# A transformer block in float32 on one core: the down projection as seven products of quarters, with its weights looked up one stage earlier

## The chip, the cores and the metric

The kernel runs on one core of a Trainium2 chip. The time is device microseconds of that core for one execution of the whole block. Before the change it was 3123.69 us (median of 3 runs, 3119.15 to 3126.1).

## What is computed

One block over 2048 tokens of width 1024: causal attention with 16 heads and rotary embedding, then a gated feed-forward part whose three weight matrices are stored as 4-bit codes with one scale for each 64 columns. The change touches the feed-forward part alone:

```python
NF4 = [-1.0, -0.6962, -0.5251, -0.3949, -0.2844, -0.1848, -0.0911, 0.0,
       0.0796, 0.1609, 0.2461, 0.3379, 0.4407, 0.5626, 0.7230, 1.0]
H, I = (1024, 2752)
W = (NF4[codes].reshape(out, in_ // 64, 64) * scales[:, :, None]).reshape(out, in_)
gate = einsum('bsh,ih->bsi', x, Wg)
up = einsum('bsh,ih->bsi', x, Wu)
inter = silu(gate) * up
return einsum('bsi,hi->bsh', inter, Wd)
...
x = x + layernorm(attention(layernorm(x)))
x = x + layernorm(ffn(layernorm(x)))
```

## The kernel before

All data are float32. A product of two float32 matrices is made of three matmuls on rounded parts (`mm3`, lines 114 to 116): each operand is split into a high and a low part (`split`: ACT copies the high part, DVE subtracts to get the low one, line 121), and high x high, high x low and low x high are added in one PSUM bank. Every such matmul is 128 x 128 by 512 columns.

The stages follow each other: queries, keys and values with attention; the output projection (`project_out`), whose rows go out to `yd` and come back to be transposed (`fill_x2`) into the four groups `x2[0..3]` of 512 tokens that stay in SBUF; gate and up; down. There are eight PSUM banks, taken in turn with `any_bank`. SBUF is cut into slots by tag (`SLOTS`): `hd` 7, `w` 3, `xc` 4, `pa` 6 of 8 KB for each partition, and `pb` 2, `f4` 4, `pw` 3, `t2` 3, `ol` 1 of 4 or 2 KB. All DMAs are issued by SP, in order. The order of the instructions on each engine is made by a scheduler when the program is built; a tile waits until a slot of its tag is free.

*Gate and up.* The 2752 inner columns are 22 tiles of 128 (`NIT`), the last of 64. One round handles one tile: `gate_up` runs over the four token groups, each with a gate product and an up product of 24 matmuls, then ACT makes Silu, DVE multiplies, the result is split, and high and low part together are stored in DRAM (`ind`). Beside that, `gate_up_weights` makes the weights of the next round in four calls of `looked_up`, into two tiles of `hd` or `pa`, so that two rounds' weights exist at a time. The last two rounds run together, group by group.

*The lookup.* `looked_up` turns 128 x 512 codes into values without a table: seven straight lines, each an ACT instruction (line 498) into a `t2` slot, an eighth line on DVE (line 493), and minima and maxima of them on DVE (lines 503 to 510), then the product with the scales (line 511). It takes 7 ACT and 10 DVE instructions, and loads of codes and scales into a `pw` slot.

*Down.* For each half of the output columns and each half of the tokens, eight banks gather eight token tiles over 22 steps (`kt`). A step loads one tile of `ind` (1 MB, `load_inter`) and multiplies it with one tile of looked-up down weights (`wd`), which are made beside these products (`down_weights`) and kept for the second token half. The last step leaves one matmul of each three out where its 64 rows hold both parts. Then `keep` copies a bank to SBUF on ACT. When both column halves of a token tile are there, `finish` loads the residual row `x1d`, makes the layer norm (bn_stats, bn_aggr and small operations on DVE, a power on GpSimd, ACT and DVE for the rows) and stores the result. In the last quarter the final four steps (`LAST`) are run bank by bank, so that `finish` of one bank lies beside the matmuls of the next.

Of the kernel before, what the change touches and what calls it, by code (L numbers as in the profile page):

```python
# [28 lines left out]
NIT = 22  # L29
EPS = 1e-5  # L30
# [12 lines left out]
L0 = (0.30380719900131226, -1.0)  # L43
L2 = (0.1301555633544922, 0.2558603286743164)
L4 = (0.09966795146465302, 0.11423042416572571)
L6 = (0.09105003625154495, 0.09105003625154495)
L8 = (0.08134990185499191, 0.07958029955625534)
L10 = (0.0918029397726059, 0.06250642240047455)
L12 = (0.12190717458724976, -0.046918854117393494)
L14 = (0.2770431637763977, -0.9393021464347839)  # L50
# [7 lines left out]
def block_kernel(ctx, tc, x, wq, wk, wv, wo, gu_codes, gu_scales, d_codes, d_scales, cos_sin, out):  # L58
# [41 lines left out]
    for ab in (L2, L4, L6, L8, L10, L12, L14):  # L100
        bias_of[ab] = const.tile([P, 1], F32, tag=f"b{len(bias_of)}", name="bias")
        G.memset(bias_of[ab], ab[1])
# [20 lines left out]
    def ln_stats(row):  # L123
        st = small.tile([P, 2, 6], F32, tag="st", name="st")
        for i in range(2):
            V.bn_stats(st[:, i, :], row[i])  # L126
        mv = small.tile([P, 2], F32, tag="mv", name="mv")
# [32 lines left out]
    ind = [[dram.tile([P, 2, 2, 512], F32, tag=f"ind{g}_{k}", name=f"ind{g}_{k}") for k in range(NIT)] for g in range(2)]  # L160
# [320 lines left out]
    def looked_up(codes, s0, s1, rows, tags=None):  # L481
# [10 lines left out]
        l0 = slot("ol" if not tags else "t2", [P, 512], F32, "l0")  # L492
        V.tensor_scalar(l0, c8.bitcast(I32), L0[0], L0[1], ALU.mult, ALU.add)
        V.tensor_scalar(c8, c8.bitcast(I32), 1.0, -8.0, ALU.mult, ALU.add)

        def line(ab):
            ln = slot("t2", [P, 512], F32, "ln")
            A.activation(ln, c8, AF.Identity, bias=bias_of[ab], scale=ab[0])  # L498
            return ln

        mp = slot("f4", [P, 2, 512], F32, "mp")
        m, p = mp[:, 0], mp[:, 1]
        V.tensor_tensor(m, l0, line(L2), ALU.min)
        V.tensor_tensor(m, m, line(L4), ALU.min)  # L504
        V.scalar_tensor_tensor(m, line(L6), 0.0, m, ALU.min, ALU.min)
        l8 = line(L8)
        V.tensor_tensor(p, l8, line(L10), ALU.max)
        V.tensor_tensor(p, p, line(L12), ALU.max)
        V.tensor_tensor(p, p, line(L14), ALU.max)
        V.scalar_tensor_tensor(m, p, 0.0, m, ALU.max, ALU.add)  # L510
# [3 lines left out]
    def gate_up_weights(it, tags=None):  # L514
        w = it_cols(it)
        wt = [slot(tag, [P, 2, 4, w], FR, "wt") for tag in ("hd", "pa" if it % 2 else "hd")]
# [30 lines left out]

    def gate_up(it, wt, w, c):
        g = any_bank()
        hl = slot("pb", [P, 2, 512], FR, "hl")  # L550

        def product(o, a):
            for k in range(KE):
                mm3(o, wt[k // 4][:, :, k % 4, a : a + P], x2[c][k], k == 0, k == KE - 1)

        product(g, 0)
        rows = P if w == 256 else D
        inter, hi = f32(hl[:rows, 1, :]), hl[:rows, 0, :]
        if w == 256:
            u = any_bank()  # L560
            product(u, P)
        else:
            u = f32(hi)
            A.copy(u, g[D:P, :])
        A.activation(inter, g[:rows], AF.Silu)
        V.tensor_tensor(inter, u, inter, ALU.mult)
        split(hi, hl[:rows, 1, :], inter)
        load(ind[c // 2][it][:rows, c % 2], f32(hl[:rows]))

    for it in range(NIT):  # L570
        if it < NIT - 2:
            for c in range(NC):
                gate_up(*todo[it], c)
        if it + 1 < NIT:
            now, steps = gate_up_weights(it + 1)
            todo.append(now)
            for step in steps:
                step()
    for c in (1, 0, 2, 3):
# [4 lines left out]
    WD_TAGS = (  # L584
        ["pa"] * 4 + ["w"] * 3 + ["pa"] + ["xc"] * 3,
        ["pa", "xc"] + ["pa"] * 4 + ["w"] * 3 + ["pa", "xc"],
    )
    LAST = 4
    SECOND = 16
    XT_TAGS = ["f4"] * 4 + ["pb"] * 2 + ["pw"] * 2  # L590
    wd = {}

    def down_weights(n, kt):

        ns = slice(n * 512, (n + 1) * 512)
        if kt % 2 == 0:
            t = slot(WD_TAGS[n][kt // 2], [P, 2, 2, 512], FR, "wd")
            wd[n, kt], wd[n, kt + 1] = t[:, :, 0], t[:, :, 1]
        t = wd[n, kt]
        rows = P if kt < NIT - 1 else D  # L600
        b1 = min(2 * kt + 1, 42)
        m = looked_up(
            d_codes[kt * P : kt * P + rows, ns], d_scales[2 * kt : 2 * kt + 1, ns], d_scales[b1 : b1 + 1, ns], rows
        )
        if rows == P:
            split(t[:, 0], t[:, 1], m)
        else:
            A.copy(t[:, 0], m)
            V.tensor_tensor(t[D:, 0], m[D:], f32(t[D:, 0]), ALU.subtract)

    def load_inter(g, kt):
        t = slot("hd", [P, 2, 2, 512], FR, "it")
        if kt < NIT - 1:
            load(f32(t), ind[g][kt])
        else:
            for a in range(2):
                load(f32(t[a * D : (a + 1) * D]), ind[g][kt][:D])
        return t

    def down(o, it_, w, tt, first, last):  # L620

        i = it_[:, tt // 4, :, tt % 4 * P : (tt % 4 + 1) * P]
        if not last:
            mm3(o, i, w, first, False)
        else:
            T.matmul(o, lhsT=i[:, 0], rhs=w[:, 0], start=False, stop=False)
            T.matmul(o, lhsT=i[:, 1], rhs=w[:, 0], start=False, stop=True)

    def keep(t, o, n):

        if t % 4 == 0:
            kept.setdefault(n, []).append(slot(("hd", "xc")[n], [P, 4, 512], F32, "kept"))
        return A.copy(kept[n][t // 4][:, t % 4], o)

    def finish(t, left, right):

        xt = slot(XT_TAGS[t % 8], [P, E], F32, "xt")
        load(xt, x1d[t * P : (t + 1) * P, :])
        _, rs, nb = ln_stats((left, right))
        for src, h in ((right, slice(512, E)), (left, slice(0, 512))):  # L640
            A.activation(xt[:, h], xt[:, h], AF.Identity, bias=nb)
            V.scalar_tensor_tensor(xt[:, h], src, rs, xt[:, h], ALU.mult, ALU.add)
            load(out[t * P : (t + 1) * P, h], xt[:, h])

    kept = {}
    last = None
    left = [(n, kt) for n in range(2) for kt in range(NIT)]

    def make(upto):
        while left and 2 * NIT - len(left) < upto:  # L650
            down_weights(*left.pop(0))

    for n in range(2):
        for g in range(2):
            os = [any_bank() for _ in range(8)]
            final = n == 1 and g == 1
            its = []
            for kt in range(NIT):
                if (n, g) == (0, 0):
                    make(kt + 1)  # L660
                elif (n, g) == (0, 1):

                    with tc.issue_after(last.ins):
                        make(NIT + min(4 + kt, SECOND))
                it_ = load_inter(g, kt)
                if final and kt >= NIT - LAST:
                    its.append(it_)
# [67 lines left out]
```

## Time and profile before

The profiled execution took 3127.5 us; its span from the first to the last instruction is 3125.7 us.

| what | value |
|---|---|
| busy: TensorE, weight loads, DVE, ACT, GpSimd | 3003.9, 2470.5, 2161.1, 1831.5, 702.8 us |
| mean granted TensorE clock | 0.982 |
| first and last matmul of gate and up (starts) | 1692.5, 2643.2 us |
| first and last matmul of down (starts) | 2643.4, 3116.4 us |
| end of the span | 3125.7 us |
| DMA traffic of the whole span | 552.31 MB, mean 177 GB/s |

How to read it: an engine's busy time is the time in which at least one of its instructions was running. Matmuls overlap each other, so their mean duration is longer than the distance from one to the next, and that distance is what a matmul costs. A row of the profile gives line, engine, operation, written and read tiles, shapes and count, then busy time and mean duration, then how long the engine had been idle before these instructions and what ended the idle time.

### The profile page before, as it was taken

Reading aid. Unit: us, or ns where it says so; the run is one execution under the profiler, and the core shown is the slowest. Engines: PE = TensorE matmul, PEld = TensorE weight load, DVE = VectorE, ACT = ScalarE, POOL = GpSimd, SP = SyncE. Lnnn points to the kernel's source line nnn. Section 1 sums busy time; section 2 is a strip of 40 time slices with the busy share of each in tenths; the row PEclk is TensorE's granted clock in tenths of the full one; section 3 lists DMA queues with packets and bytes.
Section 4 is the critical chain, followed back from the end, with each engine's and each line's share of the span. In section 5 each row is a group of like instructions: output and inputs, shape, how many; then the busy total and the mean of one; then the engine's idle time right before and its main releaser. Section 6 shows DMA issues by size and latency. Waiting matters only on the chain.

```text
span 3125.7 us, 43392 instructions
## 1 busy us (share of the span) xinstructions
PE 3003.9 (96%) x14656; PEld 2470.5 (79%) x14656; DVE 2161.1 (69%) x4428; ACT 1831.5 (59%) x3846; POOL 702.8 (22%) x888
## 2 busy tenths in 40 slices
PE   7979999999998999989988999999999999999998
PEld 6868888787877787778767888888888888888887
DVE  7457778687777777776574987666776669868322
ACT  3246667676766666676554876555665558657211
POOL 5344344343433443454222000000000000000000
PEclk9989999999999999999989999999999999999999
DMA  8777666557547656462355332222322226867785
GB/s 312 250 234 224 209 207 197 178 163 222 181 161 191 200 191 196 165 202 67 113 186 193 122 128 95 93 90 102 103 99 90 93 101 213 278 218 246 254 305 197
DMA packets 246495, 552.31 MB, mean 177 GB/s; under 512 B 20224, under 2 KB 110336, under 8 KB 219136
## 3 DMA queue, kind: packets, MB, share of 16 engines
q1 hardware_dynamic: 246272, 549.53, 53.8%
q8 instruction: 116, 1.90, 0.3%
q14 instruction: 107, 0.88, 0.1%
HBM read 403.70 MB, written 145.75 MB: 176 GB/s over the span
## 4 chain that ended last, share of the span: by engine, by line
PE 42%; DMA 3%; DVE 3%; ACT 1%; issue 1%; SPq 0%; DVEq 0%; POOLq 0%; POOL 0%; ACTq 0%
PE bk L114 13%; PE bk L116 13%; PE bk L115 13%; DMA cs<-in_d_codes 1%; DMA out<-xt 1%; PE pj L440 0%; PE pj L441 0%; PE pj L442 0%; DMA it<-ind 0%; DMA y<-yd 0%; DVE mp L511 0%; DMA cs<-in_d_scales 0%; PE pt L148 0%; DVE st L126 0%; DVE mp L504 0%
## 5 line engine op out<-in xcount | busy, mean ns | idle before, releaser
L498 ACT ACTIVATE ln<-cs,bias 128x512 f32<-128x512 f32 x910 | 611.8, 719 | 136.0 <-DVE mp L504 38.4
L114 PE MATMUL bk<-x,wt 128*128 128x512 f32 x1376 | 535.8, 390 | 0.0
L115 PE MATMUL bk<-x,wt 128*128 128x512 f32 x1376 | 535.4, 389 | 0.0
L116 PE MATMUL bk<-x,wt 128*128 128x512 f32 x1376 | 535.2, 389 | 0.0
L284 POOL TENSOR_SCALAR prob<-prob,rc 128x512 f32<-128x512 f32 (+3 forms) x640 | 408.1, 660 | 408.9 <-DVE rc L279 245.2
L262 ACT ACTIVATE prob<-s,mxs 128x512 f32<-128x512 f32 (+3 forms) x640 | 401.4, 630 | 161.2 <-DVE mxs L261 147.0
L121 DVE TENSOR_TENSOR pw<-pt,pw 128x512 fp32r<-128x512 f32 (+3 forms) x640 | 377.8, 602 | 135.1 <-ACT pw L120 133.4
L261 DVE TENSOR_REDUCE mxs<-s 128x1 f32<-128x512 f32 (+3 forms) x640 | 380.1, 602 | 96.3 <-PE s L257 57.7
L120 ACT CAST pw<-pt 128x512 fp32r<-128x512 f32 (+3 forms) x640 | 323.5, 526 | 165.4 <-PE pt L294 134.7
L132 POOL TENSOR_TENSOR rs<-ve,nhalf 128x1 f32<-128x1 f32 x64 | 40.0, 637 | 1552.2 <-DVE ve L130 1546.3
L294 PE MATMUL pt<-ident,prob 128*128 128x128 f32 x2176 | 347.1, 276 | 5.1 <-DVE pw L121 4.8
L294 PEld LDWEIGHTS pt<-ident,prob 128*128 128x128 f32 x2176 | 267.8, 142 | 59.3 <-issue 7.5
L255 PE MATMUL s<-k,q 128*128 128x512 f32 (+3 forms) x640 | 266.8, 417 | 36.9 <-ACT prob L262 35.4
L115 PEld LDWEIGHTS bk<-x,wt 128*128 128x128 f32 x1376 | 258.6, 188 | 53.9
L114 PEld LDWEIGHTS bk<-x,wt 128*128 128x128 f32 x1376 | 258.7, 188 | 53.5
L116 PEld LDWEIGHTS bk<-x,wt 128*128 128x128 f32 x1376 | 258.4, 188 | 53.7
L114 PE MATMUL bk<-wd,it 128*128 128x512 f32 x672 | 261.6, 389 | 1.2 <-DMA it<-ind 1.2
L115 PE MATMUL bk<-wd,it 128*128 128x512 f32 x672 | 261.4, 389 | 0.0
L116 PE MATMUL bk<-wd,it 128*128 128x512 f32 x672 | 261.3, 389 | 0.0
L299 PE MATMUL o<-pw,v 128*128 128x512 f32 (+3 forms) x640 | 250.6, 394 | 4.9 <-DVE pw L121 4.6
L298 PE MATMUL o<-pw,v 128*128 128x512 f32 (+3 forms) x640 | 247.1, 387 | 6.1 <-ACT pw L120 5.5
L114 PE MATMUL qkv<-xc,w 128*128 128x512 f32 x576 | 235.8, 409 | 13.0 <-ACT w L173 7.4
(124 smaller groups left out, 5514.2 us busy)
## 6 DMA issues: line engine op xcount, KB each, us to landing
xc<-xd SPq DMA_DIRECT2D x96, 1024.0 KB, 8.8
it<-ind SPq DMA_DIRECT2D x84, 1024.0 KB, 7.0
ind<-hl SPq DMA_DIRECT2D x84, 512.0 KB, 2.6
q<-qs SPq DMA_DIRECT2D x128, 256.0 KB, 7.1
cs<-in_gu_scales SPq DMA_DIRECT2D x172, 128.0 KB, 3.1
cs<-in_gu_codes SPq DMA_DIRECT2D x86, 256.0 KB, 2.9
tab<-in_cos_sin SPq DMA_DIRECT2D x32, 512.0 KB, 9.8
xd<-xr SPq DMA_DIRECT2D x16, 1024.0 KB, 6.8
```

Source lines behind the costliest of these rows:

```text
L114: r = T.matmul(o, lhsT=w[:, 0], rhs=xx[:, 0], start=first, stop=False)
L115: T.matmul(o, lhsT=w[:, 0], rhs=xx[:, 1], start=False, stop=False)
L116: T.matmul(o, lhsT=w[:, 1], rhs=xx[:, 0], start=False, stop=last)
L120: A.copy(hi, src)
L121: V.tensor_tensor(lo, src, f32(hi), ALU.subtract)
L255: mm = T.matmul(s, lhsT=q[:, 0, j * P : (j + 1) * P], rhs=k[:, b:e], start=True, stop=False)
L261: V.tensor_reduce(mx, s, AX.X, ALU.max, negate=True)
L262: A.activation(prob[i][:, j, : e - b], s, AF.Exp, bias=mx, accum_out=sums[:, j % BATCH, i : i + 1])
L284: G.tensor_scalar(p, p, rc[:, jj % BATCH, i : i + 1], 0.0, ALU.mult, ALU.add)
L294: T.transpose(pt[:, j * P : (j + 1) * P], prob[kb // 4][:, j, kb % 4 * P : (kb % 4 + 1) * P], ident)
L299: T.matmul(o[:, cs], lhsT=v[:, kb, :], rhs=pw[:, 1, cs], start=False, stop=kb == nk - 1)
L498: A.activation(ln, c8, AF.Identity, bias=bias_of[ab], scale=ab[0])
```

## The change

1. *Down as seven products of quarters (Strassen's scheme in Winograd's form).* The tokens are split by 512-token groups (even, odd), the inner tiles into tiles 0 to 10 and 11 to 21, the output columns into two halves of 512. Instead of eight products of quarters there are seven, of sums of quarters (`PRODUCTS`), each with 11 steps over eight banks. Results are gathered in SBUF quarters `u`, `c`, `v`, `d` (`evict`), partly on ACT, partly by DVE additions that read PSUM, partly by GpSimd additions.
2. *The operands are made in the gate-up stage.* Rounds alternate between tiles k and k + 11 (`PAIRS`), so that after each second round the four quarters of one k are there. GpSimd makes S1 to S4 from them, unsplit, and SP stores A11, A12, A22 and S1 to S4 in DRAM (`aq`). The quarters wait in `pb` and `f4` slots.
3. *All down weights are looked up beside gate and up*, two lookups in each round; GpSimd makes T1 to T4, and SP stores B11, B21, B22 and T1 to T4 in DRAM (`bq`). The room for them is in `f4`.
4. *In down*, `fetch` loads each step's A tile (512 KB, `f4`), and B tiles two steps at a time (512 KB, `pb`), and splits them (ACT and DVE) into `hd` and `w` slots.
5. *The lookup* has five ACT lines, three of them with two slopes (Prelu), and six DVE instructions.
6. *finish* takes bn_stats of the quarter that was complete early beforehand, and one of the two row additions goes to GpSimd. The upper rows (n = 5) use the three `pw` slots for the residual rows, the lower rows (n = 6) pairs in `xc`.

Three products have a last step of 64 rows; the matmuls are of the same length.

```diff
+PAIRS = [k // 2 + k % 2 * (NIT // 2) for k in range(NIT)]
...
+PRODUCTS = (("A11", "B11"), ("A12", "B21"), ("S2", "T2"), ("S3", "T3"), ("S1", "T1"), ("S4", "B22"), ("A22", "T4"))
...
-        l0 = slot("ol" if not tags else "t2", [P, 512], F32, "l0")
-        V.tensor_scalar(l0, c8.bitcast(I32), L0[0], L0[1], ALU.mult, ALU.add)
         V.tensor_scalar(c8, c8.bitcast(I32), 1.0, -8.0, ALU.mult, ALU.add)
         def line(ab):
             ln = slot("t2", [P, 512], F32, "ln")
-            A.activation(ln, c8, AF.Identity, bias=bias_of[ab], scale=ab[0])
+            if ab[2] == 1.0:
+                A.activation(ln, c8, AF.Identity, bias=bias_of[ab], scale=ab[0])
+            else:
+                A.activation(ln, c8, AF.Prelu, bias=bias_of[ab], scale=ab[0], alpha=ab[2])
             return ln
...
+        low = line(CODES_6_8)
+        V.scalar_tensor_tensor(m, line(CODES_9_12), CODES_9_12[3], low, ALU.add, ALU.max)
+        V.scalar_tensor_tensor(m, line(CODES_2_5), CODES_2_5[3], m, ALU.add, ALU.min)
+        V.tensor_tensor(m, m, line(CODES_0_1), ALU.min)
+        V.scalar_tensor_tensor(m, line(CODES_13_15), CODES_13_15[3], m, ALU.add, ALU.max)
         V.tensor_tensor(m, m, sc, ALU.mult)
...
 def gate_up(it, wt, w, c):
...
+        kt, later, grp, odd = it % half, it // half, c // 2, c % 2
+        if (kt, later, grp) not in rooms:
+            rooms[kt, later, grp] = slot("f4" if later else "pb", [P, 2, 512], F32, "in")
+        inter = rooms[kt, later, grp][:, odd]
...
-        split(hi, hl[:rows, 1, :], inter)
-        load(ind[c // 2][it][:rows, c % 2], f32(hl[:rows]))
+        if (later, odd) != (0, 1):
+            keep(("A11", "A12", "A22")[later + odd], inter)
+        first = rooms[kt, 0, grp]
+        if later == 0 and {(kt, grp, 0, 1 - odd)} <= have:
+            s3 = slot("ol", [P, 512], F32, "s3")
+            G.tensor_tensor(s3, first[:, 0], first[:, 1], ALU.subtract)
+            keep("S3", s3)
+        if {(kt, grp, a, b) for a in range(2) for b in range(2)} <= have:
+            second = rooms[kt, 1, grp]
+            G.tensor_tensor(first[:, 1], first[:, 1], second[:, 1], ALU.add)
+            keep("S1", first[:, 1])
+            G.tensor_tensor(first[:, 0], first[:, 1], first[:, 0], ALU.subtract)
+            keep("S2", first[:, 0])
+            G.tensor_tensor(second[:, 0], second[:, 0], first[:, 0], ALU.subtract)
+            keep("S4", second[:, 0])
...
+    for n in range(NIT):
+        if n < NIT - 2:
+            for c in range(NC):
+                gate_up(*todo[n], c)
+        if n + 1 < NIT:
+            now, steps = gate_up_weights(n + 1)
...
+        for j in range(2):
+            down_weights(n // 2, 2 * (n % 2) + j)
...
+    def fetch(a, b, kt):
+        st = slot("f4", [P, 2, 512], F32, "ast")
+        load(st, aq[a][kt])
+        ta = slot("hd", [P, 2, 2, 512], FR, "at")
+        split(ta[:, 0], ta[:, 1], st)
+        if kt % 2 == 0:
+            n = min(2, half - kt)
+            st = slot("pb", [P, 2, 512], F32, "bst")[:, :n]
+            load(st, bq[b][:, kt : kt + n])
+            b_tile[b] = slot("w", [P, 2, 2, 512], FR, "bt")
+            split(b_tile[b][:, 0, :n], b_tile[b][:, 1, :n], st)
+        return ta, b_tile[b][:, :, kt % 2]
...
+    def finish(r, lower, known, fresh, xt):
+        t = 8 * (r // 4) + 4 * lower + r % 4
+        load(xt, x1d[t * P : (t + 1) * P, :])
+        st = early_stats[known, r]
+        known, fresh = quarter[known][r], quarter[fresh][r]
+        V.bn_stats(st[:, 1, :], fresh)
+        _, rs, nb = ln_rest(st)
+        a, b = (slice(512, E), slice(0, 512)) if lower else (slice(0, 512), slice(512, E))
+        A.activation(xt[:, b], xt[:, b], AF.Identity, bias=nb)
+        A.activation(known, known, AF.Identity, bias=nb, scale=rs)
+        V.scalar_tensor_tensor(xt[:, b], fresh, rs, xt[:, b], ALU.mult, ALU.add)
+        (V if lower and r == 7 else G).tensor_tensor(xt[:, a], xt[:, a], known, ALU.add)
+        for h in (b, a):
+            load(out[t * P : (t + 1) * P, h], xt[:, h])
...
+    def evict(n, r, o):
+        q = quarter
+        if n == 0:
+            A.copy(q["u"][r], o)
+        elif n == 1:
+            V.tensor_tensor(q["c"][r], q["u"][r], o, ALU.add)
+            stats_of("c", r)
+        elif n == 2:
+            V.tensor_tensor(q["u"][r], q["u"][r], o, ALU.add)
+        elif n == 3:
+            V.tensor_tensor(q["v"][r], q["u"][r], o, ALU.add)
+        elif n == 4:
+            A.copy(q["d"][r], o)
+            G.tensor_tensor(q["u"][r], q["u"][r], q["d"][r], ALU.add)
+            G.tensor_tensor(q["d"][r], q["d"][r], q["v"][r], ALU.add)
+            stats_of("d", r)
+        elif n == 5:
+            V.tensor_tensor(q["u"][r], q["u"][r], o, ALU.add)
+            finish(r, 0, "c", "u", slot("pw", [P, E], F32, "xt"))
+        else:
+            if r % 2 == 0:
+                pair[:] = [slot("xc", [P, 2, E], F32, "xt")]
+            V.tensor_tensor(q["v"][r], q["v"][r], o, ALU.add)
+            finish(r, 1, "d", "v", pair[0][:, r % 2])
...
+    for n, (a, b) in enumerate(PRODUCTS):
+        os = [any_bank() for _ in range(8)]
...
+        for kt in range(half):
+            ab = fetch(a, b, kt)
+            rows = D if kt == half - 1 and b in ("B21", "B22", "T4") else P
+            if final and kt >= half - LAST:
+                held.append((ab, rows))
+                continue
+            for r in range(8):
+                down(os[r], ab, r, rows, kt == 0, kt == half - 1)
+        for r in range(8):
+            for i, (ab, rows) in enumerate(held):
+                down(os[r], ab, r, rows, False, i == LAST - 1)
+            evict(n, r, os[r])
```

`down_weights(kt, step)` looks up one of the four quarters of tile k: step 0 gives B11, step 1 B12 and T1 = B12 - B11, step 2 B22, T3 = B22 - B12 and T2 = B22 - T1, step 3 B21 and T4 = B21 - T2. Every T is made by GpSimd in place, and all but B12 are stored.

## The prediction, before the run

> **What bounds the kernel now.** I read the page's busy shares first, then busy time by stretch, then TensorE's own timeline, then the rows of the two last stages. The stretches decide:
>
> ```profile
> core 0: us, PE busy (x) PEld busy (x) DVE busy (x) ACT busy (x) POOL busy (x), PEclk, DMA share, GB/s
> ...
> 1400.00:1706.00 306.00, 280.10 (x1339) 228.70 (x1339) 189.29 (x414) 168.94 (x319) 93.24 (x103) 0.94 0.42 135
> 1706.00:2643.00 937.00, 932.61 (x4123) 771.60 (x4122) 697.68 (x1214) 583.73 (x941) 0.00 (x0) 1.00 0.33 110
> 2643.00:3117.00 474.00, 472.66 (x2083) 390.33 (x2081) 253.68 (x476) 208.32 (x324) 8.07 (x14) 1.00 0.73 252
> 3117.00:3126.00 9.00, 0.00 (x0) 0.00 (x0) 5.04 (x12) 2.79 (x5) 1.10 (x2) 0.74 0.58 216
> ```
>
> The rows are attention's end with the output projection, gate and up, down, and the tail after the last matmul. In gate-up and down TensorE is never idle for more than a moment, at full granted clock; DVE and ACT have room. So time there is the number of matmuls times their distance, and a removed matmul is worth its full distance.
>
> That distance is not the mean duration. The rows say 389 ns, but matmuls overlap; the timeline gives the spacing:
>
> ```profile
> L114 PE MATMUL bk<-wd,it 128*128 128x512 f32 x672 | 261.6, 389 | 1.2 <-DMA it<-ind 1.2
> L115 PE MATMUL bk<-wd,it 128*128 128x512 f32 x672 | 261.4, 389 | 0.0
> ...
> 2630.05 0.39 PE L115 MATMUL bk<-x,wt 128*128 128x512 f32 x1
> ...
> 2637.98 0.39 PE L114 MATMUL bk<-x,wt 128*128 128x512 f32 x1
> ```
>
> There are 35 matmuls from one to the other: 7.93 / 35 = 0.2266 us. The down stage agrees: 2080 matmuls x 0.2266 = 471.3 us against 472.7 busy.
>
> **What the Trainium skill says.** Perfetto Trace Analysis, Identifying the Most-Contended Engine: matmul busy time is no measure of distance to roofline, because matmuls are pipelined. This trace agrees: 389 ns long, 227 ns apart. SBUF — State Buffer, Who interferes with whom: DVE and GpSimd share a port pair, held for a whole instruction while the other blocks. Here a DVE tensor_tensor of 0.69 us took 2.32 us while GpSimd added:
>
> ```profile
> 1574.10 2.34 POOL L450 TENSOR_TENSOR x<-x,y 128x1024 f32<-128x1024 f32 x1 [2.23 <-ACT y L141]
> 1574.67 2.32 DVE L503 TENSOR_TENSOR mp<-l,ln 128x512 f32<-128x512 f32 x1 [2.00 <-ACT ln L498]
> 1577.78 0.69 DVE L504 TENSOR_TENSOR mp<-mp,ln 128x512 f32<-128x512 f32 x1 [0.79 <-ACT ln L498]
> ```
>
> This matters since the change gives GpSimd two-input work in a stage where it had none. ScalarE: Activation LUTs, Step-by-step: what each stage is for: throughput is the same for every function. For Identity (719 ns) and Silu (594 ns, from PSUM) the trace has durations; Prelu it does not show. The same page's What ACT_TABLE_LOAD costs has about 1283 ns per load, and this trace shows 1283 ns twice. The built new program also holds two loads, so Silu and Prelu don't alternate tables.
>
> **The change, part by part.**
>
> *Matmuls.* Before: 2 halves x 2 groups x 22 steps x 8 x 3 = 2112, less 32 left out at the last step = 2080. After: 7 products x 11 x 8 x 3 = 1848. 232 fewer x 0.2266 = **-52.6 us**. This is on the path, all of it.
>
> *Lookups.* The lookup row is
>
> ```profile
> L498 ACT ACTIVATE ln<-cs,bias 128x512 f32<-128x512 f32 x910 | 611.8, 719 | 136.0 <-DVE mp L504 38.4 <-DVE mp L505 36.9 <-DVE mp L507 29.2
> ```
>
> One lookup falls from 7 ACT lines and 10 DVE instructions to 5 and 6. In steady stretches ACT lines follow each other at 0.63 us and DVE instructions at 0.605 us. A round of gate-up has 192 matmuls = 43.5 us. It now makes 6 lookups instead of 4: ACT 6 x 5 x 0.63 + 4 casts x 0.52 + 4 Silus x 0.5 = 23.0 us; DVE 6 x (0.34 + 5 x 0.605) + 8 x 0.605 = 25.0 us; both below 43.5 and near the present load. The stage's total stays hidden.
>
> *The order inside a round.* Here the cover is thin. In the built order of odd rounds, ACT starts three lines of the next weights, then has the Silus of token groups 0, 1 and 2 ahead of the fourth line. The third Silu waits for its product, 5 x 5.44 = 27.2 us into the round. What follows, up to the last piece of the fourth lookup, is 22 ACT lines, 4 casts and 1 Silu = 16.4 us, and on DVE 28 x 0.605 + 2 x 0.34 = 17.6 us, with waits on the line slots: complete at 46 to 49 us. The next round starts at 43.5; its built PE order places 37 matmuls (8.4 us) ahead of the first that needs the fourth lookup, so at 51.9, and at 46.9 the low half of the third (41 to 43). Slack is about 4 us. The adds S1, S2, S4 on GpSimd start when DVE has multiplied the last group, at 44.2. The nearest rows are
>
> ```profile
> L232 POOL TENSOR_TENSOR sh<-sh,tab 128x512 f32<-128x512 f32 x64 | 95.7, 1495 | 367.5 <-DVE sh L230 175.3 <-DVE sums L276 73.3 <-DMA tab<-in_cos_sin 65.5
> L233 POOL TENSOR_TENSOR t<-t,sh 128x512 f32<-128x512 f32 x64 | 83.1, 1299 | 26.6 <-DVE t L231 14.4 <-DVE cf L273 2.8 <-DVE sm L277 2.1
> ```
>
> so 3 x 1.3 to 1.5 us, in which DVE can be held up to 4 us: just the slack. Bounds over ten such rounds: 0 and 30 us (3 each). I take **+1 us**. Below zero is excluded: TensorE has no gap there to win.
>
> *Prelu.* Lower bound the Identity's 0.72 us, upper bound twice that; I take 0.72.
>
> *Fetching.* Per step of 5.44 us the new down stage loads 512 KB of A and on average 256 KB of B = 145 GB/s, against 252 GB/s now. The splits cost ACT 1.5 x 1.05 = 1.6 us and DVE 1.5 x 1.3 = 2.0 us per step. Seven slots of finished A and four of raw A lie ahead; landing now takes 7.0 us for 1 MB. Hidden; 0 to +4 us. The two pauses of the present stage (1.2 us for `it`, 1.0 for `kept`) may go or stay: 0.
>
> *Evictions.* Banks finish 0.68 us apart and are wanted 5.44 us later. The longest queue, additions with bn_stats and two splits on DVE, ends at about 10.5 us for the last bank, which is wanted at about 10.2 or later, since the built order of TensorE runs several steps on the first banks. 0 to +1 per change of product; I take 0.
>
> *GpSimd late in down.* 16 adds x 1.3 = 21 us, against seven prefetched steps (38 us): hidden.
>
> *End of down.* The upper rows are finished through three `pw` tiles: result out (3 us), x1 in (4 to 6 us), ACT, DVE, three times over; their DVE instructions stand ahead of the split of the last B tile and of the final evictions. Counted from the first finished bank of product six, the last B tile is split at 39 us and wanted at 45; the last upper row is done near 48.5, while the first final eviction could start at 46.2. DVE then works 2.3 us per tile against TensorE's 2.7 and catches up. The SP queue is passed too: loads of the last `xt` pairs stand behind these stores. **+1.5 us**, bounds 0 and +9 (three transfers 3 us slower each).
>
> *Tail.* The last bank needs one more PSUM addition (0.69) before bn_stats, and GpSimd's add for the row before stands ahead of the power: 0.7 + 1.3 - 1.0 (one multiply-add now made elsewhere). 8.9 us becomes about 9.9: **+1 us**.
>
> *Output projection.* The waits there total some 25 us, most of it
>
> ```profile
> PE pt L148 <- DMA y<-yd: 14.4, 4, 5.8
> ...
> PE pj L440 <- ACT a L120: 7.3, 3, 4.9
> ```
>
> The code is the same but four lookups inside are shorter, and the built order moves the transposes. The transfers that end the waits stay. -8 to +6; I take **-1 us**.
>
> Sum: -52.6 + 1 + 1.5 + 1 - 1 = -50.1. The profiled execution (3127.5, span 3125.7) becomes 3077.4. It lies 3.8 above the median 3123.69, so the median becomes **3074 us**.
>
> **Rivals.**
>
> A. *Late weights.* GpSimd's adds and the slot waits fall on the fourth lookup and each of ten rounds loses 1 to 3 us, or the fetch chain loses as much: +10 to +30, near 3095. For it: the order above has TensorE short of work at every second round. Against: my chain still leaves 4 us.
>
> B. *Slower.* One mechanism: Prelu's price. 13 of the 22 ACT lines of the late window are Prelu; its ACT work ends at 44.3 and is wanted at 51.9, so 7.6 us are free. With each Prelu x us dearer, ten rounds lose 10 (13x - 7.6); the gain is gone from x = 1.0, a Prelu of 1.7 us. At 1.8 us: 10 x 6.4 = 64, near 3138. Against: the stated equal throughput.
>
> C. *The gaps of the output projection shrink* by 8 to 12 us with the shorter lookups: 3064.
>
> D. *It doesn't do what it says*: excluded for matmuls, the built program has 232 fewer.
>
> **How the numbers follow.** Forecast (3066 to 3084) 0.60; A 0.22; C 0.08; B 0.07; losses that just cancel the gain 0.03. The range 3062 to 3100 takes the forecast, most of A and half of C. A measurement tells 0.2%, 6 us: faster 0.90, same 0.03, slower 0.07.
>
> **What would show it.** Right: TensorE busy about 418 us in down at 0.227 us spacing; gate-up still near 937 us. Late weights: waits of `bk` for `wt` at every second round. B: Prelu rows above 1.4 us. End chain: DVE waiting for `xt` loads in the last 40 us. Wrong altogether: waits of `bk` for `at` or `bt` at each step.

## The result and the profile after

The changed kernel takes 3076.81 us (median of 4 runs, 3070.5 to 3079.22), the kernel before 3121.42 us on the same chip (4 runs, 3118.01 to 3126.1). The ratio is 0.985, with a 95% interval of 0.983 to 0.987: the change saves 45 us, 1.5%. The forecast was 3074 us.

The profiled execution after took 3075.66 us, its span is 3073.8 us, 51.9 less than the span before. That is 7 us more than the medians differ by, because the profiled execution before lay 6.1 us above its median of 4 runs and the one after 1.2 us below its own. First the same stretches as in the prediction, for the changed kernel (attention's end with the output projection, gate-up, down, tail; columns as there):

```profile
core 0: us, PE busy (x) PEld busy (x) DVE busy (x) ACT busy (x) POOL busy (x), PEclk, DMA share, GB/s
...
1400.00:1706.00 306.00, 287.52 (x1409) 234.29 (x1407) 190.26 (x423) 173.10 (x338) 96.48 (x105) 0.97 0.44 146
1706.00:2643.00 937.00, 928.91 (x4088) 767.38 (x4088) 644.99 (x943) 525.52 (x820) 204.86 (x135) 1.00 0.43 143
2643.00:3065.00 422.00, 420.48 (x1824) 342.49 (x1824) 195.23 (x242) 135.72 (x155) 60.06 (x48) 0.99 0.51 164
3065.00:3074.00 9.00, 0.00 (x0) 0.00 (x0) 3.61 (x8) 2.28 (x4) 3.35 (x3) 0.50 0.46 175
```

Gate-up still has a busy TensorE, though GpSimd now works there 205 us, where it had nothing. Down is shorter, and its DMA traffic is 164 GB/s instead of 252. To see where the 51.9 us went, the stretches are too coarse; TensorE's own marks are better. The changed kernel's are the starts in these rows (count, durations, first and last start, then shapes), and the last matmul ends at 3063.5:

```profile
L445 PE MATMUL pj<-wo,a x256: 387/389/796, 1405.3 to 1680.0; 128*128 128x512 f32 x128
L114 PE MATMUL bk<-x,wt x1376: 387/389/776, 1680.7 to 2632.2; 128*128 128x512 f32 x197
L114 PE MATMUL bk<-bt,at x616: 386/389/797, 2632.8 to 3062.6; 128*128 128x512 f32 x150, 64*128 64x512 f32 x4
```

The first row of the table counts from the start of the span, and all of it is in us:

| stage, from mark to mark | before | after | difference | forecast |
|---|---|---|---|---|
| up to the first matmul of the output projection | 1402.1 | 1405.3 | +3.2 | - |
| output projection, to the first matmul of gate-up | 290.4 | 275.4 | -15.0 | -1 |
| gate-up, to the first matmul of down | 950.9 | 952.1 | +1.2 | +1 |
| down, to the end of the last matmul | 473.4 | 430.7 | -42.7 | -52.6 + 1.5 |
| tail | 8.9 | 10.3 | +1.4 | +1 |

The sum is -51.9 against a forecast of -50.1. That the sum came out right is luck, since two terms missed in opposite directions: the output projection won 14 us more than forecast, and down about 8 us less than its two terms together. Both had to be explained. (The first row is no effect of the change: over all the runs below, in kernels whose code up to there is the same, this mark lay anywhere from 1395.8 to 1410.0.)

Down has 1848 matmuls, at 0.2266 us each 418.8 us; it took 430.7. The timeline of the changed kernel, TensorE first, shows one piece of the 12 us that are too many (start, duration, engine, line, operation; in brackets the idle time before it and what ended it):

```profile
2638.53 0.39 PE L116 MATMUL bk<-bt,at 128*128 128x512 f32 x1
2643.06 0.80 PE L114 MATMUL bk<-bt,at 128*128 128x512 f32 x1 [4.14 <-ACT in L574]
2643.65 0.63 PE L115 MATMUL bk<-bt,at 128*128 128x512 f32 x1
2644.08 0.63 PE L116 MATMUL bk<-bt,at 128*128 128x512 f32 x1
```

In the same timeline, ACT's instructions at that time:

```profile
2639.81 1.04 ACT L120 CAST bt<-bst 128x1024 fp32r<-128x1024 f32 x1 [2.58 <-DMA bst<-B]
2640.76 1.04 ACT L120 CAST at<-ast 128x1024 fp32r<-128x1024 f32 x1
2641.82 0.58 ACT L572 COPY u<-bk 64x512 f32<-64x512 f32 x1
2642.42 0.59 ACT L574 ACTIVATE in<-bk 64x512 f32<-64x512 f32 x1
```

The first product of down needs eight banks, and the eighth still holds the last product of gate-up, which had ended by 2633. Its copy and Silu (L572, L574) stood behind casts of fetched tiles in ACT's queue, and these waited for their transfers. TensorE was idle for 4.14 us, and the next twelve matmuls came at 0.43 us instead of 0.23. The second piece is at the end, in the weight loads of the last product (PEld):

```profile
3040.51 0.18 PEld L114 LDWEIGHTS bk<-bt,at 64*128 64x128 f32 x1 [0.35 <-issue]
3040.61 0.19 PEld L115 LDWEIGHTS bk<-bt,at 64*128 64x128 f32 x1
3040.84 0.18 PEld L116 LDWEIGHTS bk<-bt,at 64*128 64x128 f32 x1
3041.40 0.19 PEld L114 LDWEIGHTS bk<-bt,at 128*128 128x128 f32 x1 [0.37 <-issue]
```

The last inner tile has 64 rows. Where weights change from 128 to 64 rows or back, the load didn't start beside the matmul before it: PEld was idle for 0.35 and 0.37 us ahead of it. The last product works bank by bank, so each bank has one such pair of changes: its twelve matmuls take 3.15 us (from 3040.51 to 3043.66) instead of 12 x 0.2266 = 2.72. The 64-row matmuls themselves are not slow. At the end of the second product 24 of them follow each other, and from the seventh to the last (TensorE's timeline) there are 17 distances in 3.87 us, 0.228 us each:

```profile
2756.15 0.39 PE L114 MATMUL bk<-bt,at 64*128 64x512 f32 x1
...
2760.02 0.39 PE L116 MATMUL bk<-bt,at 64*128 64x512 f32 x1
```

### The profile page after: what moved, and what is told of

The parts are those of the page before. It is cut to its first block, busy times and chain, and to the rows that moved or that the text cites. A ratio compares the mean times of both kernels' runs of the same rounds, so it can differ in the third digit from the quotient of the medians.

```text
span 3073.8 us, 42810 instructions
## 1 busy us (share of the span) xinstructions
PE 2958.1 (96%) x14424; PEld 2426.6 (79%) x14424; DVE 2045.6 (67%) x3920; ACT 1700.1 (55%) x3565; POOL 960.4 (31%) x1055
## 4 chain that ended last, share of the span: by engine, by line
PE 83%; DMA 8%; DVE 4%; ACT 2%; issue 1%; POOL 1%; SPq 1%; POOLq 0%; ACTq 0%; DVEq 0%
PE bk L114 14%; PE bk L115 14%; PE bk L116 14%; PE pt L299 6%; PE qkv L114 6%; PE qkv L115 5%; PE qkv L116 5%; PE o L304 4%; PE s L260 3%; PE o L303 3%; PE s L262 3%; DMA wf<-in_wq 1%; PE pj L445 1%; PE pj L447 1%; PE pj L446 1%
## 5 line engine op out<-in xcount | busy, mean ns | idle before, releaser
L506 ACT ACTIVATE ln<-cs,bias 128x512 f32<-128x512 f32 x520 | 359.7, 716 | 109.4 <-DVE m L513 23.0
L260 PE MATMUL s<-k,q 128*128 128x512 f32 (+3 forms) x640 | 268.7, 420 | 38.1 <-ACT prob L267 36.2
L114 PE MATMUL bk<-bt,at 128*128 128x512 f32 (+1 forms) x616 | 242.1, 395 | 4.3 <-ACT in L574 4.1
L115 PE MATMUL bk<-bt,at 128*128 128x512 f32 (+1 forms) x616 | 240.7, 391 | 0.0
L116 PE MATMUL bk<-bt,at 128*128 128x512 f32 (+1 forms) x616 | 239.8, 391 | 0.0
L262 PE MATMUL s<-k,q 128*128 128x512 f32 (+3 forms) x640 | 238.6, 374 | 0.0
```

The source lines that it names most:

```text
L114: r = T.matmul(o, lhsT=w[:, 0], rhs=xx[:, 0], start=first, stop=False)
L115: T.matmul(o, lhsT=w[:, 0], rhs=xx[:, 1], start=False, stop=False)
L116: T.matmul(o, lhsT=w[:, 1], rhs=xx[:, 0], start=False, stop=last)
L260: mm = T.matmul(s, lhsT=q[:, 0, j * P : (j + 1) * P], rhs=k[:, b:e], start=True, stop=False)
L506: A.activation(ln, c8, AF.Prelu, bias=bias_of[ab], scale=ab[0], alpha=ab[2])
```

## The experiments

### The kernel again, and the two pieces of down

The first group ran on one chip. The changed kernel itself:

> The changed kernel unchanged, as the measure for the other runs of this call. From its first profile: 430.7 us from the first matmul of the down stage to its last eviction, one idle stretch of 4.1 us of TensorE ahead of a Silu at the hand-over, time about 3076 us. If the stall at the hand-over is a matter of chance between executions, it is absent here; if it comes from the order of ACT's queue, it is here again at 3 to 5 us.

It took 3075.54 us (4 runs, ratio to before 0.985, 0.983 to 0.987). The stall was there again at 4.28 us, with the same twelve slow matmuls; down took 431.2 us. So it is not chance; that the order of ACT's queue is its cause is for the third run to show.

Full rows in each product:

```diff
-            rows = D if kt == half - 1 and b in ("B21", "B22", "T4") else P
+            rows = P
```

> Every product of the down stage multiplies 128 rows; the 64 rows that products 2, 6 and 7 leave out are zeros, so the sum is the same. The number of matmuls is the same. Theory (a switch between weights of 64 and of 128 rows costs TensorE a weight load that does not overlap): the twelve matmuls of a bank in the last product go from 3.15 back to 2.72 us, and the down stage is shorter by 8 x 0.43 + 2 x 0.4 = 4.2 us, so 426.5 us. Rival (the 64-row matmuls themselves are slow, or the last product waits for its evictions): the banks of the last product keep 3.15 us and the stage keeps 430.7 us.

Down took 423.6 us, 7.6 less than in the repeated run of the changed kernel. The weight loads of the last product are evenly spaced:

```profile
3040.29 0.19 PEld L114 LDWEIGHTS bk<-bt,at 128*128 128x128 f32 x1
3040.51 0.19 PEld L115 LDWEIGHTS bk<-bt,at 128*128 128x128 f32 x1
3040.74 0.19 PEld L116 LDWEIGHTS bk<-bt,at 128*128 128x128 f32 x1
```

Of the 7.6 us, some 3.4 belong to the hand-over, not to this edit: the idle time there was 0.9 us less (3.75 us ended by the Silu), and the twelve matmuls after it ran at 0.23 us at once instead of 0.43, with the granted clock at 1.00. What is left, some 4.2 us, is the price of the changes of rows, as expected. (The run takes the 64-row matmuls away together with the changes and so can't tell the two apart; the 24 in a row above can.) The median fell by 11.6 us, to 3063.98 (ratio 0.9825, 0.980 to 0.985), which is more than the stage can give; in the profiled executions another 5.7 us lie before the output projection, in the spread named above.

The fetches behind the last Silu:

```diff
-            ab = fetch(a, b, kt)
+            if n == 0 and kt >= 4:
+                with tc.issue_after(last.ins):
+                    ab = fetch(a, b, kt)
+            else:
+                ab = fetch(a, b, kt)
```

(`last` is the Silu that `gate_up` now returns.)

> The fetches of the first product's tiles from the fifth on are put behind the last Silu of gate-up in the order of issue. Theory (the Silu stood behind casts on ACT that waited for fetched tiles): TensorE's 4.1 us of idle time at the hand-over and the twelve slower matmuls after it (2.4 us) go, the down stage takes 424 us instead of 430.7, the time is 6 to 7 us lower. Rival (the transfers themselves are late, so the stall only changes its place): the Silu is in time, but TensorE waits as long for an at or bt tile within the first product, and the stage keeps 430.7 us within 1.5.

TensorE did not wait once at the hand-over. For this kernel, the stretch from the first to the last matmul of down:

```profile
2625.20:3048.40 423.20, 423.19 (x1849) 344.99 (x1847) 201.41 (x243) 139.90 (x160) 62.40 (x48) 1.00 0.53 171
```

423.2 us instead of 431.2 and 430.7: the stall and the slow matmuls are gone, and no wait for `at` or `bt` took their place. The rival falls, and the order of ACT's queue is shown as the cause. Time 3061.51 us (ratio 0.982, 0.980 to 0.984), 14 us below the repeated run of the changed kernel where 6 to 7 were expected: down gave 8.0, and in the profiled execution the output projection began 10.2 us earlier, again in that spread.

Both, and one addition of the tail on VectorE:

```diff
-        (V if lower and r == 7 else G).tensor_tensor(xt[:, a], xt[:, a], known, ALU.add)
+        (V if lower and r >= 6 else G).tensor_tensor(xt[:, a], xt[:, a], known, ALU.add)
```

> Both edits, and the addition of the second-last row of the last product on VectorE instead of GpSimd. Theory: the gains add: down stage 420 us, against 418.8 us for 1848 matmuls at 0.2266 us, and the tail after the last matmul 9 instead of 10.3 us; time about 3064 us, 12 us below the changed kernel. Rival: with the idle time gone the fetches bound the stage (they must bring 150 GB/s on average), so waits for at or bt take back half of it and the time stays above 3068 us.

Down took 419.04 us, and TensorE has no wait in it: 1848 x 0.2266 = 418.8, so the forecast's term for the matmuls was exact, and all that was missing is found. The tail missed its number: 10.1 us instead of the expected 9. The addition had left GpSimd, but it now stood on VectorE ahead of the statistics of the last row. Time 3061.99 us (ratio 0.981, 0.979 to 0.983).

### What the shorter lookup is worth

Two runs ask why the output projection became shorter, and a third what the lookup does for the rounds. The kernel before with the new lookup alone (the function `line`, the combining instructions and their slots as in the change, everything else as before):

> The kernel before with the five-line lookup alone; the down stage stays at 2080 matmuls and its old order. Theory (the first gate-up matmul comes 11.8 us earlier because the first four lookups, made beside the output projection, are shorter): first gate-up matmul at 1680 to 1684 us instead of 1692.5, time 3110 to 3114 us. Rival (the change of issue order around it, not the lookup, moved it): first gate-up matmul stays at 1692 and the time at 3119 to 3124 us.

The stage's part held: the output projection took 275.0 us, as after the change, and its waits for `y` fell from 14.4 to 2.6 us. But the time did not follow: 3118.98 us against 3120.73 (ratio 0.999, 0.998 to 1.0003). Down gave a half of it back: 481.2 us from mark to mark instead of 473.4, with these waits in it:

```profile
PE bk L111 <- DMA it<-ind: 5.0, 4, 2.0
PE bk L111 <- ACT hl L559: 1.1, 1, 1.1
```

Why these loads came later was not tried. The other half is there in the profiled executions, whose spans differ by 8.8 us, but of the medians 1.7 is left, and the interval reaches from 7 us won to 1 lost. So the shorter lookup by itself wins nothing that could be measured.

The other way round, the changed kernel with its four lookups beside the projection made longer:

```diff
+        if tags:
+            V.tensor_tensor(m, m, line(CODES_0_1), ALU.min)
+            V.scalar_tensor_tensor(m, line(CODES_13_15), CODES_13_15[3], m, ALU.add, ALU.max)
+            for _ in range(2):
+                V.tensor_tensor(m, m, m, ALU.max)
         V.tensor_tensor(m, m, sc, ALU.mult)
```

> The changed kernel with the four lookups beside the output projection made as long as the old ones: two lines more on ScalarE and four operations more on VectorE each, which repeat what is there, so the values stay. Theory (length of these lookups): the wait for y from yd comes back, first gate-up matmul at 1688 to 1693 us, time +8 to +12 us. Rival (order or slots): first gate-up matmul within 2 us of 1680.7, time +0 to +2 us.

In its list of waits in this stage (engine, what it waited for, us in total, times, longest), the wait of before is back, where the changed kernel has 0.6 us:

```profile
PE pt L151 <- DMA y<-yd: 15.7, 3, 7.9
PE pj L445 <- ACT a L120: 6.7, 3, 4.0
```

The output projection took 287.9 us; in all the runs with short lookups there it took 274.2 to 277.6, and before the change 290.4. So the lookups' length sets this stage. How it does so is open, because the scheduler builds another order for another length. Between its groups of transposes TensorE runs 80, 32, 48, 42, 18, 64 and 37 matmuls of the projection in both kernels with short lookups there, and 81, 36, 65 before and 77, 37, 66 here. No run keeps the order and changes the length alone.

The time rose by 4.5 us over the repeated run of the changed kernel (3079.99 us, ratio 0.986), below the 8 to 12 expected. From the first matmul of the projection on, the two profiled executions differ by 10 us: 13.0 lost in the stage, 0.7 won back in gate-up and 2.2 in down, where the stall was shorter. What part of this the time keeps stays open.

The same lengthening for all other lookups (`if not tags:`; there are 82 of gate-up and 44 of down, fewer than the expectation says):

> The changed kernel with all other lookups, those of gate-up and of down, made as long in the same way; the 84 lookups of down and 84 of gate-up each gain 2 x 0.72 us on ScalarE and about 4 x 0.6 us on VectorE. Theory (the odd rounds have only 2 to 4 us of slack for their fourth lookup, so the shorter lookup is what makes room for the down lookups): the fourth gate-up lookup comes 6 to 10 us later and TensorE waits 3 to 7 us for weights in each of ten odd rounds, time +30 to +70 us. Rival (the order in which the lookups are started gives way, the slack is the whole round): waits below 1 us a round, time within 5 us of the changed kernel.

3209.58 us: 2.8% slower than the kernel before (ratio 1.028, 1.025 to 1.031). The gain of the seven products is gone, and 89 us more. The middle of gate-up in this kernel:

```profile
2100.00:2500.00 400.00, 369.14 (x1558) 294.96 (x1557) 376.01 (x551) 267.72 (x406) 100.67 (x50) 0.98 0.36 121
```

VectorE is busy for 376 of 400 us. Over the whole of gate-up TensorE waits 67.3 us for `wt` of ACT and 15.5 for that of VectorE. The expectation was too low since it looked at one late lookup in every second round alone; here VectorE is busy for some 90% or more of every round from the third on, and TensorE waits in each. This is the most important of the runs: the down lookups fit beside gate-up because the lookup is short. With lookups as long as these, the change is a loss.

### How much room the rounds have

One and two more operations on VectorE in each lookup of the rounds:

```diff
+        if not tags:
+            for _ in range(1):
+                V.tensor_tensor(m, m, m, ALU.max)
         V.tensor_tensor(m, m, sc, ALU.mult)
```

> The changed kernel with one operation more on VectorE in each lookup of gate-up and of down (the maximum of a tile with itself, so the values stay). Theory (the fourth gate-up lookup of an odd round has about 4 us of slack, and the four lookups ahead of its use gain 4 x 0.66 = 2.6 us): waits for weight tiles rise by less than 1 us a round, time +0 to +8 us. Rival (VectorE's mean load counts, 30 us of a round of 43.5): no change within 3 us.

3073.37 us (ratio 0.984, 0.983 to 0.986): no change. Gate-up took 953.1 us, and TensorE waited for `wt` in none of its rounds but the last two. (At the hand-over it was idle for 8.2 us instead of 4.9, but the output projection began 7.8 us earlier than in the repeated run of the changed kernel.)

> Two such operations in each lookup. Theory (slack of about 4 us): four lookups gain 5.3 us, the weights come 1 to 3 us late in each of ten odd rounds, time +10 to +30 us over the changed kernel, with TensorE's waits for wt that much longer. Rival (mean load): VectorE has 30 + 6 x 1.3 = 38 us of work in 43.5, and the time stays within 4 us.

3092.47 us (ratio 0.990, 0.989 to 0.9915), 19 us more than with one. By the marks gate-up took 972.4 us instead of 952.1, but 6.5 us of it are idle time at the hand-over, which here lies ahead of the first matmul of down. Gate-up and down together took 15 us more than in the changed kernel and 12 more than with one operation; the rest of the 19 is, in the profiled executions, 8 us before the output projection. TensorE waits for `wt` in nine rounds, every second one, 0.2 to 1.1 us in each (and once, 2.9 us, near the end):

```profile
2009.74 0.50 PE L114 MATMUL bk<-x,wt 128*128 128x512 f32 x1 [0.69 <-ACT wt L120]
2011.42 0.50 PE L116 MATMUL bk<-x,wt 128*128 128x512 f32 x1 [0.26 <-DVE wt L121]
```

The time is in the theory's range, but the waits are shorter than its 1 to 3 us, and they are not at the place that the prediction named. Count the rounds from 0. The prediction's thin place is where an even round needs the fourth lookup, 37 matmuls in. In the changed kernel it was right about that place. Round 8 starts at 2043.46, its matmul that needs the high half comes 37 x 0.2266 us later, at 2051.84, and the one for the low half at 2052.52; the two halves are written here (ACT's and VectorE's timelines):

```profile
2047.05 0.62 ACT L120 CAST wt<-m 128x512 fp32r<-128x512 f32 x1 [0.36 <-DVE m L514]
2050.34 0.68 DVE L121 TENSOR_TENSOR wt<-m,wt 128x512 fp32r<-128x512 f32 x1
```

That leaves 4.2 us for the high half, the predicted slack, and 1.5 for the low one. But the runs with more operations don't test this slack. The scheduler built a new order for each of them: by the semaphores in the traces, the matmul that waits for the fourth lookup's high half stands 37 matmuls into the even rounds in the changed kernel, 47 with one operation more and 61 with two, and TensorE waits there in neither.

The waits of the run with two are in the odd rounds, 18 matmuls in. The fourth lookup for these is made in the even round before. In the changed kernel it was some 10 us early (written by 38 us into that round, wanted at 47.6), and with two operations more up to 0.8 us late. Two rounds of the changed kernel, one odd and one even (7 and 8), show why:

```profile
2000.00:2043.50 43.50, 43.50 (x194) 36.02 (x193) 19.50 (x32) 17.05 (x28) 7.16 (x5) 1.00 0.30 105
2043.50:2087.00 43.50, 43.50 (x194) 36.02 (x193) 40.20 (x58) 31.36 (x49) 11.35 (x7) 1.00 0.50 165
```

and rounds 6 and 7 with two operations more:

```profile
1961.29:2004.81 43.52, 43.52 (x193) 36.05 (x192) 42.91 (x63) 26.95 (x43) 14.37 (x7) 1.00 0.46 147
2004.81:2049.86 45.05, 44.10 (x194) 35.88 (x192) 31.97 (x52) 20.81 (x34) 9.63 (x5) 1.00 0.37 122
```

VectorE has 19.5 us of work in one round and 40.2 in the next, where the prediction had 25.0 in each; with two operations more the heavier round is full, 42.9 of 43.5 us. So the rival's mean load says nothing of it.

The sums S and T on VectorE (eight `G.tensor_tensor` become `V.tensor_tensor` in `gate_up` and `down_weights`):

> The changed kernel with the sums of quarters S1 to S4 and T1 to T4 on VectorE instead of GpSimd: about six more operations of 0.66 us a round on VectorE, and no addition of GpSimd beside the lookups. Theory (the additions are hidden where they are, and VectorE in every second round is nearly full, 40 of 43.5 us): the weights come later and the time rises by 3 to 25 us. Rival (GpSimd's additions hold up VectorE by up to 4 us a round[...]): the fourth lookup comes earlier, TensorE's waits for wt go, time -1 to -3 us.

The time fell by more than the rival said: 3068.85 us (ratio 0.982, 0.980 to 0.9835), 7 us less than the repeated run of the changed kernel and 10 by the ratios. The waits for `wt` are gone, but they were 0.9 us. Most of the gain is at the hand-over, where the idle time ended by the Silu is 0.6 us with this order of issue; down took 424.2 us. What is instructive is VectorE's busy time in gate-up. From the stretches, first the changed kernel:

```profile
1706.00:2633.00 927.00, 923.18 (x4065) 763.30 (x4066) 639.52 (x938) 520.26 (x814) 202.54 (x134) 1.00 0.42 141
```

and with the sums on VectorE:

```profile
1706.00:2633.00 927.00, 923.90 (x4071) 764.68 (x4070) 640.15 (x1071) 514.25 (x821) 3.02 (x6) 0.99 0.43 142
```

VectorE has 133 instructions more in this stretch and the same busy time. The additions that moved took 88 us there, 0.69 each. So GpSimd's 203 us of additions had spared VectorE nothing: beside them its other instructions were longer by as much. One row of the lookup shows it, from the groups of VectorE in this stretch (count, then busy time and mean ns), the changed kernel first:

```profile
L512 DVE TENSOR_TENSOR mb<-mb,ln 128x512 f32<-128x512 f32 x44 | 50.5, 1147 | 4.8 <-ACT ln L506 0.5
```

and the kernel with the sums on VectorE:

```profile
L512 DVE TENSOR_TENSOR mb<-mb,ln 128x512 f32<-128x512 f32 x44 | 30.2, 687 | 1.5
```

### The best version

The two edits of down without that of the tail:

> The fetches from the fifth on behind the last Silu of gate-up, and 128 rows in every product; the tail stays as it is. Theory: down stage 419 to 420 us as in the run with the third edit, tail 10.3 us, time 3061 to 3065 us. Rival (a part of the gain of the three edits came from the tail): 2 us or more above the run with three edits.

3065.4 us (ratio 0.981, 0.980 to 0.983); down took 419.04 us. The ratio is the same as with three edits, so the third gave nothing that could be measured.

And with the sums on VectorE too:

> The two edits (fetches behind the last Silu, 128 rows in every product) with the sums of quarters S and T on VectorE too. Theory (GpSimd's additions cost VectorE as much as they spare it, and the run with these sums on VectorE won by its hand-over alone): nothing left to win beside the two edits; down stage 419 to 420 us, no wait for wt over 0.5 us, time 3058 to 3066 us, equal to the two edits within 4 us. Rival (the sums on VectorE win by themselves): 3050 to 3057 us.

The stretch of down in this kernel:

```profile
2627.90:3047.00 419.10, 419.09 (x1849) 346.67 (x1848) 200.15 (x244) 138.84 (x157) 55.40 (x43) 1.00 0.53 171
```

3059.48 us (ratio 0.981, 0.979 to 0.983), TensorE busy throughout down, and in gate-up and down only one wait above noise, of 2.5 us for `x` at the start. Its ratio equals that of the two edits, as the theory said: nothing was left to win there. Both kernels are about 12 us (0.4%) below the change, and 59 us below the kernel before.

## Why the prediction was right, and where it wasn't

*Matmuls, -52.6 us.* Right as a price: with the two edits down falls to 419.0 us, 1848 x 0.2266. In the changed kernel 12 us stood beside it, for which the prediction had 1.5.

*Where the 12 us came from.* The step that failed is "Evictions", taken at 0, together with the line of "Fetching" that the pauses of the present stage "may go or stay: 0". They looked at the inside of down and at the changes from product to product, which indeed cost nothing, and not at the change from gate-up to down, where the last Silu takes part in the same queue as the casts of the first fetches. That was 7.5 us (4.1 of them idle, most of the rest slower matmuls). The other 4.2 us are missing from "Matmuls": 64-row matmuls were counted at the common distance, and nothing was put for the changes of rows.

*Output projection, -1 us.* The step "the transfers that end the waits stay" failed. The runs say the opposite: with short lookups these waits are 0.6 and 2.6 us, with long ones 14.4 and 15.7. The DMA named as the releaser was only the last link; the lookups' length decides when it is needed and when it starts, through their running time or through the order built from it. Rival C had the mechanism at 8 to 12 us; the stage won 15. It counts as the second mis-sized term, and it hid the first.

*The order inside a round, +1 us.* No loss came, as said, and the chain's end was well worked out: 47.7 us into the round for the high half and 51.0 for the low, forecast 46 to 49. The size is not shown: gate-up grew by 1.2 us, and in the runs whose rounds have the same code it took 950.1 to 952.4. Nor is the slack of 4 us tested, since the built order gave way wherever lookups were made longer. Rival A came as a time (3092 us with two more operations per lookup, the rival's 3095), but by another way: VectorE full in the even rounds, and late weights in the odd ones.

*Lookups hidden.* Right in effect. VectorE's load per round was 29.9 us on average instead of 25.0, with 40.2 in every second one. The missing part is the time that GpSimd's additions held VectorE up, which the prediction put at a place (up to 4 us at a round's start) and left out of this sum. Without them the sum is good: with the sums on VectorE its other work in the stretch is 640.2 - 88 = 552 us in 927, or 25.9 in a round.

*Prelu, 0.72 us.* Right: the line with one slope and those with two have the same price. Two counts given ahead of the run were wrong: four of the five lines have two slopes, not three, and so 17 or 18 of the 22 late lines, not 13. Rival B fell by the price alone. (By its own terms, 27.2 + 16.4, ACT's late work ended at 43.6 us, not at 44.3.) The rows of ACT in the changed kernel, two slopes first, then one:

```profile
L506 ACT ACTIVATE ln<-cs,bias 128x512 f32<-128x512 f32 x520 | 359.7, 716 | 109.4 <-DVE m L513 23.0
L504 ACT ACTIVATE ln<-cs,bias 128x512 f32<-128x512 f32 x130 | 93.9, 722 | 28.3 <-DVE mb L510 17.0 <-DVE m L510 9.3
```

*Fetching, 0.* Right; in the best version TensorE never waits for `at` or `bt` at 171 GB/s. *End of down, +1.5.* TensorE did not wait there at all, so 0. *Tail, +1.* It was +1.4, and its working (GpSimd's addition ahead of the power) is what the trace shows; taking that addition away won only 0.2 us, since VectorE then has it in the same place.

## What to carry to other kernels

Look at each place where one stage hands its banks over to the next, and at what stands ahead of the last instruction of the old stage in its in-order queue: prefetching for the new stage can hold up the end of the old one. A part of a change that wins nothing alone can be what makes the other parts possible; here the shorter lookup is worth nothing measurable by itself, and lengthening it within the change cost 134 us. When a list of waits names a DMA, ask what set the time of its start before calling the wait fixed. And where a scheduler builds the order, a longer instruction changes the order too: look up where the waiting instruction now stands before reading such a run as a test of a slack.

## What the hardware showed beside that

- A change between 64 and 128 weight rows cost about 0.2 us each time (0.43 us for the pair in a bank of the last product). Multiplying by 64 rows of zeros instead was cheaper, since matmuls of 64 rows came at the same distance as those of 128 (0.228 and 0.227 us).
- After the idle time at the hand-over, matmuls came at 0.426 us until the clock was back, in runs with 2.7 (after another 0.9 a little earlier), 4.1, 4.3, 6.5 and 15.9 us of idle time, and not in one with 3.75. The Trainium skill, TensorE: Matmul & The Clock Gate, Part 1: The HAM clock gate, has 426.7 ns for 512 columns at the throttled clock, and a free-running window of some 3.4 us after which an idle array is throttled. The spacing agrees, and so does the window: in each trace all changes of the granted clock lie multiples of 3.41 us apart. But the window need not be idle throughout. Laid over all 14 traces from the last transpose to the last matmul, windows with 1.99 us of idle time or more were followed by the half clock (19 of them), and those with 1.91 or less were not. The 3.75 us once cost nothing because they fell on two windows, 1.91 and 1.85 us in each. Here the measurement decides. The changed kernel (columns as above), the window of its stall and the two at half clock:

```profile
2638.31:2641.72 3.41, 0.61 (x3) 0.18 (x1) 1.01 (x2) 1.91 (x2) 1.30 (x1) 1.00 0.74 241
2641.72:2648.55 6.83, 5.49 (x13) 4.38 (x14) 3.99 (x4) 2.29 (x4) 4.41 (x3) 0.50 0.90 308
```

  and the kernel with full rows, the two windows of its stall:

```profile
2630.51:2633.93 3.42, 1.51 (x6) 0.90 (x6) 1.81 (x2) 2.15 (x3) 1.17 (x1) 1.00 0.86 293
2633.93:2637.34 3.41, 1.56 (x7) 1.31 (x8) 2.62 (x3) 2.33 (x4) 0.64 (x1) 1.00 0.78 241
```

- The same skill, SBUF — State Buffer, Who interferes with whom, says that DVE instructions with two SBUF inputs and GpSimd's reads block each other. This case adds the price: additions of 1.3 to 1.7 us on GpSimd saved VectorE nothing at all beside its lookups (639.5 against 640.2 us of busy time).
